# Transposing gathered expert rows on VectorE and ScalarE instead of TensorE, in a float32 mixture-of-experts kernel

## The chip, the cores and the metric

The kernel runs on one core of a Trainium2 chip. The metric is device time in microseconds (us) of one execution. Before the change it is 930.4 us, the median of three runs (930.36, 930.40, 931.57). In the text PE is TensorE, DVE is VectorE, ACT is ScalarE, POOL is GpSimd and SP is SyncE.

## What is computed

Four sequences of 1024 tokens of width 512 each pass through one linear layer, chosen per sequence from 64 by a category number. A router then sends every token to the best of 8 experts, at most 512 tokens to each. An expert is two matrices with a ReLU between them (512 to 2048 to 512). Its output, scaled by the router's probability, is added to the token's original `x`. Everything is float32.

```python
xc = einsum('bsd,bdh->bsh', x, W[cat]) + b[cat][:, None, :]
probs = softmax(xc @ Wr);  eidx = argmax(probs);  p_tok = probs[eidx]
rank = how many earlier tokens chose the same expert;  keep = rank < 512
for e in range(8):
    xe = xc[tokens of e]                      # 512 x 512
    h  = maximum(xe @ W1[e], 0)               # 512 x 2048
    y[tokens of e] += (h @ W2[e]) * p_tok
out = x + y
```

## The kernel before

**Two stages.** The first stage (up to about 149 us) transposes `x`, computes the linear layer and the router, and writes the layer's result to two DRAM tensors `xc_dram` (left and right half of the columns). It also writes, for each slot of each expert, which token sits there. The second stage works through experts `e = 0` to `7`, each some 96 us long.

**Seven products instead of eight.** All large products use a Strassen-Winograd scheme: the operands are cut in quarters, DVE forms sums and differences of quarters (`sums`, `differences`), and seven products, numbered `k = 1` to `7`, are accumulated in three PSUM banks called x, y and z. Product 1 opens bank x; ACT takes a snapshot of the bank (line 761), and products 6 and 7 are then accumulated onto it, with a snapshot after each. So product 6 may only begin when snapshot `s1` has been copied, 7 when `s6` has, and 4 when `s7` has. Each bank has two buffers.

**One expert.** Its 512 rows are gathered by POOL (`gather`, line 691) into four tiles of 128 rows, in two halves of 256 columns each. PE transposes them (`transpose_rows`, line 719) into a PSUM tile, ACT copies that to the tile `xe` (line 720; for expert 0 DVE does), and DVE adds three blocks of differences (lines 729 to 733). The first layer then runs over four groups `g = 0..3` of 512 hidden columns, with seven products of 1.73 us of PE time in each group: 1, 2, then 4 and 3 of the group before, then 6, 5, 7. `first_layer` ends with the bank totals on DVE (line 765), the ReLU on ACT (line 766, and line 773 for product 4) and, after product 3, the DVE sums of `h` (lines 160 to 163). Of the second layer three products run whole (`second_layer(e, 1)`, `6`, `7`, each 6.9 us of PE time), and products 2, 5, 3 and 4 are cut in quarters once more and run as 7 small products each (`small`, `inner_product`, line 856, 0.89 us each), after DVE has formed their `inner_sums`. Results are added to the tile `residual` (gathered rows of the original `x`) by `add`, a DVE `scalar_tensor_tensor` (line 791), and POOL scatters the finished rows to the output (line 889).

**What sets the order.** PE and SP run in the order of the program text (`manual_schedule`). On ACT, DVE and POOL a planner decides at build time: it takes the earliest instruction in the program that it believes to be ready. Each engine then runs its list strictly in that order. `behind` and `issue_after` force a place after a given instruction, and `soon` (`high_priority`) puts an instruction ahead of others that are ready. `fetch(e)`, called in group 1 of expert `e`, gathers the residual rows of `e` and then the rows of expert `e + 1`. For expert 0 the groups 0 and 1 are interleaved, so its `fetch` comes late, and at that time three large copies of `x` to the output (line 920) are under way.

**Where the transposes of the next expert stand.** They are woven between the small products of the present one by `ahead`: one tile before product (2,1), two before (2,4), one after (5,2).

```python
second_layer(e, 6)
inner_sums(e, 5)
ahead(0)
small(*[(2, q) for q in (1, 5, 2, 6, 3, 7)])
ahead(1, 2)
small((2, 4))
inner_sums(e, 3)
second_layer(e, 7)
inner_sums(e, 4)
small((5, 5), (5, 2))
ahead(3)
```

**The start.** SP issues the four loads of the first `x` chunk, then (line 211) the first weights, whose address depends on the category number; ACT issues the router weights and the clearing of `slots`. PE runs three idle matmuls (`keep_warm`, each two passes) before the first transposes of `x`.

Of the kernel before, what the change touches and what calls it, by code (L numbers as in the profile page):

```python
# [8 lines left out]
F32 = mybir.dt.float32  # L9
# [7 lines left out]
P = 128  # L17
# [5 lines left out]
def kernel(  # L23
# [29 lines left out]
    W1G = 3  # L53
    NS = E * SC
    Q = 32
    ROW = 2
# [5 lines left out]
    w1p = ctx.enter_context(tc.tile_pool(name="w1p", bufs=W1G))  # L62
    xg = ctx.enter_context(tc.tile_pool(name="xg", bufs=SC))

# [5 lines left out]

    latest = [None]

    def behind(f, *at):
# [9 lines left out]
    def unordered(group, ins):  # L83
# [8 lines left out]
    make_identity(nc, ident)  # L92
    idle = const.tile([P, D], F32, name="idle")
    nc.vector.memset(idle, 0.0)
    wr_sb = const.tile([P, KC, Q], F32, name="wr_sb")
    nc.vector.memset(wr_sb, 0.0)
    nc.scalar.dma_start(
        out=wr_sb[:, :, 0:E], in_=wr.rearrange("(kc p) e -> p kc e", p=P)
    )
    zeros = const.tile([P, T * ROW // P], F32, name="zeros")  # L100
    nc.vector.memset(zeros, 0.0)
    slots = dram.tile([T, ROW], F32, name="slots")
    nc.scalar.dma_start(out=slots.rearrange("(p s) r -> p (s r)", p=P), in_=zeros)
    before = const.tile([P, P], F32, name="before")
    make_upper_triangular(nc, before, diag=False)
    ones = const.tile([P, P], F32, name="ones")
    nc.gpsimd.memset(ones, 1.0)
# [15 lines left out]
    AHEAD = GT // 2  # L123
    scan = [const.tile([P, AHEAD + GT, E], F32, name=f"scan_{i}") for i in range(2)]
    for t in scan:
        nc.vector.memset(t, 0.0)
    wrc = [const.tile([P, KC, Q], F32, name=f"wrc_{b}") for b in range(B)]
    for t in wrc:
# [60 lines left out]
    with (  # L189
# [54 lines left out]

        def load_x(c):
            t = xin.tile([P, XT, D], F32, tag="x", name=f"x_{c}")
            n = 1 if c == 0 else XT
            for j in range(0, XT, n):
                nc.sync.dma_start(
                    out=t[:, j : j + n, :],  # L250
                    in_=xf[c * CT + j * P : c * CT + (j + n) * P, :].rearrange(
                        "(j p) d -> p j d", p=P
                    ),
                )
            xrows[c] = t
# [365 lines left out]
        with tc.manual_schedule(engines={mybir.EngineType.PE, mybir.EngineType.SP}):  # L621
            load_x(0)
            load_batch(0)
            load_x(1)
            load_batch(1)
            load_x(2)
            load_batch(2)
            keep_warm(ps_t, 3)
            for i in range(XT):
                transpose_x(0, i)  # L630
            for b in range(B):
                for i, product in enumerate(ORDERS[b]):
                    linear(*(b, *product)[-3:])
                    for f, *at in loads.get((b, i), []) + beside.get((b, i), []):
                        f(*at)
# [7 lines left out]
        for row, *ops in ((src_row, float(T - 1), ALU.add, ALU.min), (dst_row, None, ALU.add)):  # L643
            nc.gpsimd.tensor_scalar(
                row.rearrange("p (e c) -> p e c", c=SC), token, FAR, *ops
            )


# [33 lines left out]
    def gather(e, pool, sources, into, at):  # L682

        n = D // len(sources)
        for j, source in enumerate(sources):
            for c in range(SC):
                if j == 0:
                    into[e * SC + c] = pool.tile(
                        [P, D], F32, tag="rows", name=f"rows_{e * SC + c}"
                    )  # L690
                nc.gpsimd.indirect_dma_start(  # L691
                    out=into[e * SC + c][:, j * n : (j + 1) * n],
                    out_offset=None,
                    in_=source,
                    in_offset=bass.IndirectOffsetOnAxis(ap=at[:, c : c + 1], axis=0),
                )

    def fetch(e):

        at = rowp.tile([P, 2 * SC], I32, tag="at", name=f"at_{e}")  # L700
        n = min(2 * SC, NS - e * SC)
        nc.vector.tensor_copy(at[:, 0:n], src_row[:, e * SC : e * SC + n])  # L702
        gather(e, xr, [xf], residual, at[:, 0:SC])
        if e + 1 < E:
            gather(e + 1, xg, xc_dram, rows, at[:, SC : 2 * SC])

    def transpose_rows(e, c, parts=range(2)):

        if e not in xes:
            xes[e] = xep.tile([P, 7, HK, HC * P], F32, tag="xe", name=f"xe_{e}")  # L710

        t = xes[e]
        r = rows[e * SC + c]
        half, at = divmod(c, HC)
        n = len(parts)
        lo = parts[0] * HK
        ps = ps_e.tile([P, KC, P], F32, tag="t", name=f"ps_e_{e}_{c}_{lo}")
        for kc in range(n * HK):
            nc.tensor.transpose(ps[:, kc, :], r[:, (lo + kc) * P : (lo + kc + 1) * P], ident)
        (nc.vector.tensor_copy if e == 0 else nc.scalar.copy)(  # L720
            t[
                :, 2 * half + parts[0] : 2 * half + parts[0] + n, :, at * P : (at + 1) * P
            ].rearrange("p b k n -> p (b k) n"),
            ps[:, 0 : n * HK, :],
        )
        if c == SC - 1:
            b11, b21, b12, b22, t1, t2, t4 = (t[:, k, :, :] for k in range(7))
            if 0 in parts:
                nc.vector.tensor_tensor(t1, b12, b11, ALU.subtract)
            if 1 in parts:  # L730
                nc.vector.tensor_tensor(t2, b22, t1, ALU.subtract)
                nc.vector.tensor_tensor(b12, b22, b12, ALU.subtract)
                nc.vector.tensor_tensor(t4, b21, t2, ALU.subtract)

# [5 lines left out]
    def first_layer(e, g, k):  # L740
# [16 lines left out]
        if k in (1, 6, 7):  # L757
            banks[key, k] = snap.tile(
                [P, HB, HC * P], F32, tag=f"s{k}", bufs=2, name=f"s{k}_{e}_{g}"
            )  # L760
            nc.scalar.copy(banks[key, k], ps)  # L761

# [23 lines left out]

    def add(e, ps, half, at, columns):

        row = residual[e * SC + half * HC + at][:, columns]
        with tc.high_priority():  # L790
            nc.vector.scalar_tensor_tensor(  # L791
                row, ps, table[:, half * HC + at, e, 0:1], row, ALU.mult, ALU.add
            )

    def second_layer(e, k):
# [55 lines left out]
    def inner_product(e, k, q):  # L851
# [13 lines left out]
        half, part = CORNERS[k][0]  # L865
        if len(CORNERS[k]) == 1:
            lo = part * HD + n * P
            add(e, ps, half, at, slice(lo, lo + P))
        else:
            if (e, k) not in whole:  # L870
                whole[e, k] = snap.tile([P, HC, HD], F32, tag="whole", name=f"p{k}_{e}"), set()
            t, begun = whole[e, k]
            into = t[:, at, n * P : (n + 1) * P]
            if (at, n) in begun:
                soon(nc.vector.tensor_tensor, into, ps, into, ALU.add)
            else:
                nc.scalar.copy(into, ps)
            begun.add((at, n))
            banks[e, k, "parts"] = banks.get((e, k, "parts"), 0) + 1
            if banks[e, k, "parts"] == 7:  # L880
                for half, part in CORNERS[k]:
                    for i in range(HC):
                        add(e, t[:, i, :], half, i, slice(part * HD, (part + 1) * HD))

# [37 lines left out]
    with tc.manual_schedule(engines={mybir.EngineType.PE, mybir.EngineType.SP}):  # L922
        gather(0, xg, xc_dram, rows, src_row)

        for part, half, then in (
            ([0], 0, [(0, 1)]),
            ([0], 1, [(1, 1), (0, 5), (1, 5)]),
            ([1], 0, [(0, 2)]),
            ([1], 1, [(1, 2)]),
        ):  # L930
# [6 lines left out]
        for e in range(E):  # L937
            for g in range(NG):
# [7 lines left out]
                first_layer(e, g, 1)  # L946
                first_layer(e, g, 2)
                between(e, g)
                first_layer(e, g, 6)
                first_layer(e, g, 5)  # L950
                first_layer(e, g, 7)
            second_layer(e, 1)
# [7 lines left out]
            def small(*turns):  # L960
                for k, q in turns:
                    inner_product(e, k, q)

            def ahead(*tiles):
                for c in tiles:
                    if e + 1 < E:
                        transpose_rows(e + 1, c)

            second_layer(e, 6)
            inner_sums(e, 5)  # L970
            ahead(0)
            small(*[(2, q) for q in (1, 5, 2, 6, 3, 7)])
            ahead(1, 2)
            small((2, 4))
            inner_sums(e, 3)
            second_layer(e, 7)
            inner_sums(e, 4)
            small((5, 5), (5, 2))
            ahead(3)
            small(  # L980
# [37 lines left out]
```

## Time and profile before

| what | value |
|---|---|
| median of three runs | 930.4 us |
| the profiled execution's own time | 930.86 us |
| its span in the trace | 929.1 us |
| first stage | 0 to about 148.8 us |
| one expert in the steady state (293.46 to 389.70) | 96.24 us |
| granted PE clock | 0.998 |
| transposes of gathered rows, line 719 | 128 instructions, 16 for each expert |
| copies of them on ACT, line 720 | 28, mean 588 ns |
| busy in the span: DVE, ACT, POOL | 70%, 21%, 20% |

A group line of the profile names the line, the engine, the operation, the tile written and the tiles read, the shapes and the count; then its busy time and the mean duration; then how long the engine idled before such instructions and for what. Since matmuls are pipelined, the duration of one of them is longer than the distance from its start to the start of the next. The cost of a matmul is read from the starts in the timeline.

### The profile page before, as it was taken

To read this page: it belongs to the slowest core of one execution; us is meant where nothing else is said; L and a number is where in the kernel's file an instruction comes from. 1 tells how busy PE (TensorE), PEld (TensorE's weight loads), DVE (VectorE), ACT (ScalarE), POOL (GpSimd) and SP (SyncE) were. 2 spreads that over 40 slices of the span, in tenths; PEclk is the share of its full clock that TensorE was granted. 3 is DMA by queue.
4 is the path that set the end of the run, shared out by engine and by line. 5 is a ranking of instruction groups with operands and counts; after the bars stand their busy time and mean duration, and the time that the engine had idled before them with its cause. 6 is when DMAs were issued, how large, how long until landed. Compare 5 with 4: busy or idle time off the path is not lost.

```text
span 929.1 us, 13272 instructions
## 1 busy us (share of the span) xinstructions
PE 915.9 (99%) x5318; PEld 817.5 (88%) x5318; DVE 654.9 (70%) x1222; ACT 193.5 (21%) x350; POOL 181.7 (20%) x173
## 2 busy tenths in 40 slices
PE   9999999999999999999999999999999999999996
PEld 6788787889988998899889988999889988998886
DVE  4656684589549954987488847883789368945793
ACT  3323200321132103210331023112311132113200
POOL 0043443060141013201230024001500150012001
PEclk9999999999999999999999999999999999999999
DMA  8475223992372118310841085106520562044001
GB/s 299 157 242 167 81 80 117 343 379 90 100 254 100 46 61 266 127 47 21 275 152 46 1 277 164 58 1 227 182 91 2 202 202 90 2 154 159 1 1 46
DMA packets 95727, 123.32 MB, mean 133 GB/s; under 512 B 8516, under 2 KB 83268, under 8 KB 95474
## 3 DMA queue, kind: packets, MB, share of 16 engines
q1 hardware_dynamic: 85634, 97.54, 31.5%
q0 software_dynamic: 9216, 24.85, 8.1%
q8 instruction: 42, 0.69, 0.3%
q10 hardware_dynamic: 816, 0.08, 0.1%
q14 instruction: 19, 0.16, 0.1%
HBM read 105.96 MB, written 25.23 MB: 141 GB/s over the span
## 4 chain that ended last, share of the span: by engine, by line
PE 64%; issue 18%; DVE 13%; POOL 3%; DMA 1%; ACT 0%; POOLq 0%; DVEq 0%
PE hx L746 19%; PE hy L746 9%; PE yx L856 7%; PE xcx_lin L488 6%; PE hz L746 5%; PE yx L803 4%; PE yy L856 3%; DVE rows L791 2%; PE xcy_lin L488 2%; POOL rows L691 2%; DVE h L160 2%; DVE h L161 2%; PE ps_xT L273 1%; PE xcz_lin L488 1%; DVE h L163 1%
## 5 line engine op out<-in xcount | busy, mean ns | idle before, releaser
L746 PE MATMUL hx<-xe,w 128*128 128x256 f32 x1024 | 237.7, 379 | 1.2 <-DVE xe L720 1.0
L746 PEld LDWEIGHTS hx<-xe,w 128*128 128x128 f32 x1024 | 193.8, 190 | 27.7 <-DVE xe L720 1.2
L889 POOL DMA_INDIRECT out_dram<-rows,dst_row x32 | 32.0, 999 | 465.3 <-DVE rows L791 428.6
L746 PE MATMUL hy<-xe,w 128*128 128x256 f32 x512 | 120.6, 379 | 0.0
L803 PE MATMUL yx<-w_b,h 128*128 128x256 f32 x512 | 113.1, 379 | 0.0
L746 PEld LDWEIGHTS hy<-xe,w 128*128 128x128 f32 x512 | 97.3, 190 | 13.2
L803 PEld LDWEIGHTS yx<-w_b,h 128*128 128x128 f32 x512 | 96.7, 190 | 12.8
L761 ACT COPY s<-hx 128x512 f32<-128x512 f32 x96 | 55.8, 582 | 222.7 <-PE hx L746 222.7
L765 DVE TENSOR_TENSOR h<-hy,s 128x512 f32<-128x512 f32 x64 | 44.1, 688 | 76.0 <-PE hy L746 51.7
L766 ACT ACTIVATE h<-h 128x512 f32<-128x512 f32 x96 | 60.5, 630 | 150.7 <-DVE h L765 150.7
L856 PE MATMUL yx<-w_b,h 128*128 128x128 f32 x640 | 83.4, 275 | 0.7 <-DVE rows L791 0.6
L791 DVE SCALAR_TENSOR_TENSOR rows<-yx,table,rows 128x128 f32<-128x128 f32 (+1 forms) x160 | 59.9, 398 | 30.8 <-PE yx L856 30.7
L856 PEld LDWEIGHTS yx<-w_b,h 128*128 128x128 f32 x640 | 77.3, 192 | 1.1 <-DVE rows L791 1.0
L691 POOL DMA_INDIRECT rows<-in_x_dram,at x32 | 45.2, 1412 | 145.4 <-DVE at L702 106.2
L691 POOL DMA_INDIRECT rows<-xc_dram,at x56 | 58.4, 1043 | 21.4 <-issue 14.3
L746 PE MATMUL hz<-xe,w 128*128 128x256 f32 x256 | 60.6, 379 | 0.6 <-DVE xe L720 0.6
L765 DVE TENSOR_TENSOR h<-hz,s 128x512 f32<-128x512 f32 x32 | 22.0, 688 | 55.4 <-PE hz L746 55.4
L803 PE MATMUL yx<-w_t,h 128*128 128x256 f32 x256 | 56.6, 379 | 0.0
L460 POOL DMA_INDIRECT slots<-row,dest x32 | 36.3, 1136 | 96.4 <-DVE dest L456 87.9
L746 PEld LDWEIGHTS hz<-xe,w 128*128 128x128 f32 x256 | 48.5, 190 | 7.4 <-DVE xe L720 0.9
L803 PEld LDWEIGHTS yx<-w_t,h 128*128 128x128 f32 x256 | 48.6, 190 | 6.6
L856 PE MATMUL yx<-w_t,h 128*128 128x128 f32 x384 | 52.1, 279 | 0.4
(160 smaller groups left out, 1244.3 us busy)
## 6 DMA issues: line engine op xcount, KB each, us to landing
w<-in_L_ffn_W_dram SPq DMA_DIRECT2D x64, 512.0 KB, 4.3
w_b<-in_L_ffn_W_dram SPq DMA_DIRECT2D x32, 1024.0 KB, 10.9
x<-in_x_dram SPq DMA_DIRECT2D x7, 1024.0 KB, 8.7
xc_dram<-s SPq DMA_DIRECT2D x22, 256.0 KB, 2.7
out_dram<-in_x_dram SPq DMA_DIRECT2D x2, 2816.0 KB, 20.3
cw<-in_L_cond_W_dram SPq DMA_DIRECT2D x3, 1024.0 KB, 10.6
out_dram<-in_x_dram SPq DMA_DIRECT2D x1, 2560.0 KB, 12.2
xc_dram<-xc SPq DMA_DIRECT2D x8, 256.0 KB, 2.3
```

The costliest lines, as they stand in the source:

```text
L160: eng.tensor_tensor(s1, a21, a22, ALU.add)
L460: nc.gpsimd.indirect_dma_start(out=slots, out_offset=bass.IndirectOffsetOnAxis(ap=dest[:, j : j + 1], axis=0), in_=row[:, j, :], in_offset ...
L488: nc.tensor.matmul(ps[:, j, :], lhsT=left[:, kc, j * P : (j + 1) * P], rhs=right[k][:, kc, :], start=((k in OPENS or (b, k) == (LATE, 3)) ...
L691: nc.gpsimd.indirect_dma_start(out=into[e * SC + c][:, j * n : (j + 1) * n], out_offset=None, in_=source, in_offset=bass.IndirectOffsetOnA ...
L746: nc.tensor.matmul(ps[:, j, :], lhsT=w1s[e, g][:, LEFT[k], kc, j * P : (j + 1) * P], rhs=xes[e][:, RIGHT1[k], kc, :], start=(k in OPENS an ...
L761: nc.scalar.copy(banks[key, k], ps)
L765: latest[0] = nc.vector.tensor_tensor(into, ps, part, ALU.add)
L766: nc.scalar.activation(into, into, AF.Relu)
L791: nc.vector.scalar_tensor_tensor(row, ps, table[:, half * HC + at, e, 0:1], row, ALU.mult, ALU.add)
L803: nc.tensor.matmul(ps[:, at, :], lhsT=hs[e][:, m // HB, LEFT[k], m % HB, at * P : (at + 1) * P], rhs=w2s[e][RIGHT2[k]][:, m, :], start=(k ...
L856: nc.tensor.matmul(ps, lhsT=left[:, g, :], rhs=right[:, g, :], start=(q in OPENS and g == 0), stop=(q == LAST[BANK[q]] and g == NG - 1), s ...
L889: nc.gpsimd.indirect_dma_start(out=of, out_offset=bass.IndirectOffsetOnAxis(ap=dst_row[:, n : n + 1], axis=0), in_=residual.pop(n), in_off ...
```

## The change

Expert 0's rows are still transposed by PE. For experts 1 to 7 PE no longer takes part:

- `regroup(e + 1, a)` is called four times in the last group of expert `e`. Each call issues four ACT copies. One copy moves 32 partitions of the gathered rows (512 elements in each) to another 32 partitions of a new tile `strips`. All sixteen together put 32x32 blocks where a blockwise transpose needs them.
- `turn(e + 1)` transposes the 32x32 blocks with four DVE instructions of 128x512 elements, straight into `xe`. `sum_xe` then forms the three difference blocks as before.
- The eight gathers of expert `e + 1` go to one tile with one buffer, and `fetch` issues them before the residual gathers of `e`, not after.
- `second_layer(e, 7)` moves ahead of small product (2,4).
- Small products of 2, 3 and 4 are no longer added to `residual` one by one. Of seven, three are copied by ACT to a buffer `whole`, three are added to it by DVE, one is added directly; the buffer is then added to `residual` in two pieces. Adds straight from PSUM keep their high priority, those from the buffer lose it.
- Snapshots `s1` and `s7` have one buffer instead of two.
- At the start ACT's queue issues the four loads of the first `x`, then the router weights and the clearing of `slots`; SP goes straight to the weights. `keep_warm` runs two idle matmuls instead of three. Constants of the first stage move to a pool `early` that is closed before the second.

```diff
+    early = early_on.enter_context(tc.tile_pool(name="early", bufs=1))
...
-            load_x(0)
+            load_x(0, nc.scalar)
             load_batch(0)
+            nc.scalar.dma_start(
+                out=wr_sb[:, :, 0:E], in_=wr.rearrange("(kc p) e -> p kc e", p=P)
+            )
+            nc.scalar.dma_start(out=slots.rearrange("(p s) r -> p (s r)", p=P), in_=zeros)
...
-            keep_warm(ps_t, 3)
+            keep_warm(ps_t, 2)
...
-        gather(e, xr, [xf], residual, at[:, 0:SC])
         if e + 1 < E:
             gather(e + 1, xg, xc_dram, rows, at[:, SC : 2 * SC])
+        gather(e, xr, [xf], residual, at[:, 0:SC])
...
+    def regroup(e, a):
+        if (e, "strips") not in rows:
+            rows[e, "strips"] = xep.tile(
+                [P, KC, SC, VB, V], F32, tag="strips", name=f"strips_{e}"
+            )
+        r = rows[e, "all"][a * V : (a + 1) * V].rearrange("p s (k b v) -> p s k b v", b=VB, v=V)
+        for b in range(VB):
+            into = rows[e, "strips"][b * V : (b + 1) * V, :, :, a, :]
+            with tc.issue_after(snapped[0].ins):
+                nc.scalar.copy(into.rearrange("p k s v -> p s k v"), r[:, :, :, b, :])
+
+    def turn(e):
+        t = rows.pop((e, "strips"))
+        for half in range(2):
+            for j in range(2):
+                nc.vector.transpose(
+                    xe_of(e)[:, 2 * half + j, :, :],
+                    t[:, j * HK : (j + 1) * HK, half * HC : (half + 1) * HC, :, :].rearrange(
+                        "p k s a v -> p k (s a v)"
+                    ),
+                )
...
-                [P, HB, HC * P], F32, tag=f"s{k}", bufs=2, name=f"s{k}_{e}_{g}"
+                [P, HB, HC * P], F32, tag=f"s{k}", bufs=1 + (k == 6), name=f"s{k}_{e}_{g}"
             )
-            nc.scalar.copy(banks[key, k], ps)
+            snapped[0] = nc.scalar.copy(banks[key, k], ps)
...
+        single = len(CORNERS[k]) == 1
+        if single and q == 4:
+            add(e, ps, half, at, columns(n * P, P))
         else:
...
+            if (at, n) in done:
                 soon(nc.vector.tensor_tensor, into, ps, into, ALU.add)
             else:
                 nc.scalar.copy(into, ps)
+            done.append((at, n))
+            if not single:
+                if len(done) == 7:
+                    for corner, part in CORNERS[k]:
+                        for i in range(HC):
+                            add(e, t[:, i, :], corner, i, columns(0, HD), urgent=False)
+            elif at == 1 and done.count((1, 1)) == 2:
+                add(e, into, half, 1, columns(P, P), urgent=False)
+            elif at == 0 and done.count((0, 0)) == done.count((0, 1)) == 2:
+                add(e, t[:, 0, :], half, 0, columns(0, HD), urgent=False)
...
                 first_layer(e, g, 1)
                 first_layer(e, g, 2)
+                if e + 1 < E and g == NG - 1:
+                    regroup(e + 1, 0)
                 between(e, g)
-                first_layer(e, g, 6)
-                first_layer(e, g, 5)
-                first_layer(e, g, 7)
+                for i, k in enumerate((6, 5, 7)):
+                    first_layer(e, g, k)
+                    if e + 1 < E and g == NG - 1:
+                        regroup(e + 1, i + 1)
...
             inner_sums(e, 5)
-            ahead(0)
             small(*[(2, q) for q in (1, 5, 2, 6, 3, 7)])
-            ahead(1, 2)
+            second_layer(e, 7)
             small((2, 4))
             inner_sums(e, 3)
-            second_layer(e, 7)
             inner_sums(e, 4)
+            if e + 1 < E:
+                turn(e + 1)
             small((5, 5), (5, 2))
-            ahead(3)
+            if e + 1 < E:
+                sum_xe(e + 1)
```

## The prediction

> **What bounds the kernel.** I read the page first: the busy shares, the granted clock and the chain that ended last.
>
> ```profile
> span 929.1 us, 13272 instructions
> PE 915.9 (99%) x5318; PEld 817.5 (88%) x5318; DVE 654.9 (70%) x1222; ACT 193.5 (21%) x350; POOL 181.7 (20%) x173
> PEclk9999999999999999999999999999999999999999
> PE 64%; issue 18%; DVE 13%; POOL 3%; DMA 1%; ACT 0%; POOLq 0%; DVEq 0%
> ```
>
> PE is busy throughout at full clock. A busy PE could still hide gaps, so I went on to the stretches of single experts. Columns: length, then busy time and count for PE, weight loads, DVE, ACT and POOL, then clock, DMA share, GB/s.
>
> ```profile
> 389.70:485.94 96.24, 96.19 (x561) 87.67 (x561) 70.88 (x126) 19.85 (x36) 17.43 (x16) 1.00 0.36 119
> 871.00:929.10 58.10, 49.81 (x337) 46.34 (x335) 38.39 (x77) 3.51 (x8) 3.99 (x4) 0.97 0.05 19
> ```
>
> A steady expert has 0.05 us of idle PE in 96.24. So time is saved only by taking instructions from PE, and lost only where PE gets a new wait. DVE (70.88) and ACT (19.85) have room on average; whether they have it at the right moment is the question.
>
> **What the transposes cost PE.** From PE's timeline, small products (2,7), two transposed tiles, and (2,4):
>
> ```profile
> 411.70 1.06 PE L856 MATMUL yx<-w_b,h 128*128 128x128 f32 x8
> 412.60 1.04 PE L719 MATMUL ps_e<-ident,rows 128*128 128x128 f32 x8
> 413.47 1.06 PE L856 MATMUL yx<-w_b,h 128*128 128x128 f32 x8
> ```
>
> Durations overlap, so I take starts: eight transposes hold PE for 413.47 − 412.60 = 0.87 us, 0.109 each. An expert has 16 (1.74 us), seven experts 112: **−12.2 us**.
>
> The Trainium skill ("VectorE: DVE Perf Modes", The three transpose paths, and its rules for kernel authors) speaks against the change: a full 128x128 transpose belongs on TensorE, at 390 ns in bf16, since VectorE turns only 32x32 blocks. Its 390 ns would make 112 x 0.39 = 43.7 us gained; it is the time of one alone, and the row shows 0.109 us in a stream. The row decides. The rule also leaves out which engine is full; its warning about 32x32 blocks is paid here by ACT's copies.
>
> **The work that replaces them.** The nearest rows (all 512 elements per partition):
>
> ```profile
> L720 ACT COPY xe<-ps_e 128x512 f32<-128x512 f32 x28 | 15.7, 588 | 80.2 <-PE ps_e L719 80.2
> L731 DVE TENSOR_TENSOR xe<-xe 128x512 f32<-128x512 f32 x8 | 5.5, 692 | 0.3
> ```
>
> *ACT.* Sixteen copies of 512 elements per partition. At 588 ns that is 9.4 us per expert, less four removed copies (2.35), plus nine small-product copies at 266 ns (2.4): 29 of 94 us busy. Fewer partitions should not shorten a copy; strides in runs of 32 might lengthen it. Bounds 0.5 to 1.2 us; I take 0.59. Their place matters, because PE waits for snapshots (ACT's timeline, group 3):
>
> ```profile
> 482.57 0.59 ACT L761 COPY s<-hx 128x512 f32<-128x512 f32 x1 [0.42 <-PE hx L746]
> 486.03 0.59 ACT L761 COPY s<-hx 128x512 f32<-128x512 f32 x1 [2.87 <-PE hx L746]
> ```
>
> These are `s6` and `s7`. `s1` ends at 476.57; four copies fill 476.6 to 478.9, and the next ReLU starts at 478.94 anyway. `s6` stays at 482.57, needed by product 7 at 484.05. Eight copies follow (483.2 to 487.9), so `s7` ends near 488.5 instead of 486.6; product 4 of group 3 needs it only at 492.68. No PE wait: **0**. If this cover goes, it costs what the slower rival below works out.
>
> *DVE.* Four transposes at the row's 0.69 (0.60 apart) add 2.4 us. The lower bound is 0.5 each; the upper, twice the row, adds 2.4 us more. The seven adds (348 ns) of each of products 2, 3, 4 become one add, three sums (286 ns), and two adds from the buffer (348 and 482): 2.03 instead of 2.44 us, −1.2 per expert. From 429 to 444 us DVE idles half the time, and `xe` is needed only at 439. **0** either way.
>
> *Banks.* The ACT copies and short sums release PSUM sooner. Product (5,1) needs the bank of `second_layer(7)`; its four adds ended 2.2 us after that layer, and (2,4), (5,5), (5,2) lie between now (2.7 us). Expert 7, with no transposes to cover it, waited 0.25 us at (2,7) and 0.83 at (2,4); now `second_layer(7)` precedes (2,4): **−0.8**, bounds 0 and −1.1. Tiny waits of at most 0.4 us per expert elsewhere I leave (bounds ±2 in all).
>
> *Answered shortly.* One buffer for `s1` and `s7`: their readers end before the next snapshot; in expert 0 group 1's `s1` must wait for the total at 159.6 to 160.3, and its next product comes at 163.6, so 0. The `early` pool's readers end before `xe` is first written at 148, so 0. Scatters and the end of the kernel do not move.
>
> **The start.**
>
> ```profile
> 1.14 1.81 SPq L249 DMA_DIRECT2D x<-in_x_dram  x4
> 3.99 1.56 SPq L211 DMA_DIRECT2D cw<-in_L_cond_W_dram  x3
> 5.88 0.23 PEld L273 LDWEIGHTS ps_xT<-ident,x 128*128 128x128 f32 x1 [0.52 <-issue]
> 12.18 0.69 DVE L502 TENSOR_TENSOR s<-xcx_lin,cb 128x512 f32<-128x512 f32 x1 [0.64 <-DMA cb<-in_L_cond_b_dram]
> ```
>
> The first transposes follow the idle matmuls, not the load. One idle matmul less is two passes of 0.855 us, 1.7 us. ACT issues six DMAs at about 0.45 us (0.7 to 3.4), then loads its table (1.28): free before the first copy. SP loses 1.81 us of issuing, but its next instruction still waits for the category number, so weights, bias and all later loads on SP come 0 to 1 us earlier. The bias holds the fourth row and, behind it on DVE, the sums that PE's product at 14.64 needs; the gain cannot much exceed the bias's shift.
>
> Here the skill's page "TensorE: Matmul & The Clock Gate" (The HAM clock gate) weighs against the cut: warm-up is some 3.4 us of busy time, not a number of matmuls, so transposes moved forward run cold. The trace agrees in part: the first ones took 421 ns, later ones 273. By the row alone the gain is 1.7; by the rule half the 16 transposes (0.9 us) run at half speed and 0.8 is left. I take **−0.9**, bounds 0 and −1.7.
>
> **Expert 0, the new wait.**
>
> ```profile
> 187.72 1.75 POOL L691 DMA_INDIRECT rows<-in_x_dram,at  x1 [31.81 <-issue]
> 203.74 0.87 DVE L791 SCALAR_TENSOR_TENSOR rows<-yx,table,rows 128x256 f32<-128x256 f32 x2
> 206.82 7.07 PE L803 MATMUL yx<-w_t,h 128*128 128x256 f32 x32
> 209.13 0.69 DVE L161 TENSOR_TENSOR h<-h 128x512 f32<-128x512 f32 x1
> 210.65 1.19 POOL L691 DMA_INDIRECT rows<-xc_dram,at  x1 [4.62 <-DMA rows<-in_x_dram,at]
> 203.19 11.29 DMA rows<-xc_dram,at
> ```
>
> For later experts gathers land in about 3.8 us, and there is time: the last row gather would issue near 372 and land near 376, ACT wants it at 380; residuals land near 383, DVE wants them at 396. Here gathering begins at 187.7 under copies of `x`: the third gather landed at 210.6 (the fifth row shows who waited for it), the fourth by 212.1, the ninth (last row) at 214.5. With rows first, the eight row gathers hold the bytes of the former four and land near 211.5; the first two residual tiles near 214. But DVE wants these at 203.74, and everything behind the add on DVE waits too: the total of product 3, then the sums (209.13, ending 209.8) that `second_layer(0, 6)` needs for its last quarter at 206.8 + 5.2 = 212.0. DVE's chain would shift by 214.5 − 204.6 = 9.9 us; 2.2 us of slack and 0.6 of idle DVE come off: PE waits about 7 us. If the planner puts that add behind the sums, the wait is 0 to 2. ACT's copies can block too: if they stand ahead of the two ReLUs of products 4 and 3 (207.7), those start at 211.5 + 16 x 0.55 = 220.3 and PE waits about 11. Bounds 0 and 12; I take **+6**, near the add's row and a little below, for the order is unknown.
>
> **The sum.** 930.86 (profiled execution: span 929.1 and 1.76 around it) − 12.2 − 0.9 − 0.8 + 6 = 923.0. The median lies 0.46 lower: **922.5 us**.
>
> **Rivals.**
>
> *No wait in expert 0.* The planner takes other ready work first on DVE and ACT, or loads come earlier. For it: ready work waits at 203 to 209 (weight sums, totals). Against: the add has high priority, and a planner cannot know the slow landings. 930.4 − 13.9 = **916.5 us**.
>
> *The full block on ACT in expert 0.* 16 copies ahead of the ReLUs: 930.4 − 13.9 + 11 = **927.5 us**. For it: the copies stand earlier in the program than these ReLUs. Against: the planner may already expect the rows late.
>
> *Slower: copies too slow on ACT, in every expert.* `s7` stands behind eight copies. From 483.16 to 492.68 there is room for 8c + 0.8, so PE waits once a copy takes c > 1.09 us; the gain of 7.9 us that is left in the forecast is eaten when the wait is 1.1 us per expert, at c = 1.23. At c = 1.6 the wait for `s6` (1.3 us) and for `s7` (4.8) are 6.1 us in each of seven experts: 922.5 + 43 = **965 us**. For it: copies across partitions in runs of 32 appear in no row. Against: 588 ns for 512 elements is a rate per element, and nothing suggests twice that.
>
> **Numbers.** Forecast (a wait of 4 to 9 us) 0.45, no wait 0.30, full block 0.15, slow copies 0.10. A measurement here tells 0.2%, 1.9 us, from no change. Faster takes the first two and half the third: 0.82. Same: 0.06, slower: 0.12. The range runs from the rival without a wait, with the start and small waits at their good ends (912.5), to the full block with unlucky small terms (930); left out are the slow copies and edges.
>
> **What would show it.** Line 719 with 16 instructions instead of 128. Experts 1 to 6 at about 94.5 us, with PE idle near 0. Copies of `strips` at 0.55 to 0.65 us, DVE transposes at 0.6 to 0.7. A PE gap near 210 to 220 us, and DVE waiting for a residual DMA before it (or ACT for the rows). Product (0,0,1) of the first stage near 8.5 us instead of 9.4. I am wrong if a steady expert is not shorter by about 1.7 us, or if PE waits for `s6` or `s7`.

## The result, and the profile after

The changed kernel takes 937.6 us, the median of four runs (936.94 to 938.49), against 930.7 in runs of the kernel before on the same chip. The ratio is 1.0073, with a 95% interval of 1.0056 to 1.0091: slower by about 7 us. The forecast was 922.5 us, with a range of 912.5 to 930.

Below are the lines of the changed kernel's page that answer to those shown of before.

```profile
span 935.2 us, 13219 instructions
PE 902.6 (97%) x5204; PEld 807.9 (86%) x5204; DVE 660.5 (71%) x1226; ACT 264.9 (28%) x506; POOL 176.9 (19%) x173
...
PEclk9999999978999999999999999999999999999999
...
PE 93%; DVE 2%; DMA 2%; POOL 1%; issue 1%; ACT 0%; POOLq 0%; DVEq 0%
```

PE's busy time fell by 13.3 us (915.9 to 902.6), and yet the span grew by 6.1. So PE stands idle somewhere. The clock row says where to look: the slices of some 23 us that are not full are the ninth and the tenth, 187 to 234 us. That is expert 0. A steady expert and the last part, by the stretches view (columns as before: length, busy time and count of PE, weight loads, DVE, ACT, POOL; clock, DMA share, GB/s):

```profile
313.18:407.40 94.22, 94.22 (x546) 86.07 (x545) 71.90 (x127) 29.73 (x58) 16.91 (x16) 1.00 0.38 123
878.40:935.20 56.80, 49.43 (x337) 46.30 (x335) 37.01 (x74) 5.89 (x17) 3.99 (x4) 0.98 0.05 19
```

There the change does what it was forecast to do, and a little more: 94.22 us for an expert instead of 96.24, with PE never idle, and 56.80 instead of 58.10 at the end. The view of waits (total, times, longest) has one long wait of PE:

```profile
PE hx L787 <- ACT s L802: 21.4, 1, 21.4
```

PE waits once, for a snapshot of ACT, and longer than the whole steady gain. The timeline of that place (start, duration, engine, line, operation, tiles; in brackets the idle time before it and its releaser):

```profile
186.34 1.81 POOL L704 DMA_INDIRECT rows_of<-xc_dram,at  x1 [31.73 <-DVE w L163]
188.50 0.58 ACT L814 ACTIVATE h<-hx 128x512 f32<-128x512 f32 x1
...
199.86 0.95 POOL L704 DMA_INDIRECT rows_of<-xc_dram,at  x1 [0.30 <-issue]
...
211.25 2.50 ACT L747 COPY strips<-rows_of 32x512 f32<-32x512 f32 x4 [22.17 <-DMA rows<-in_x_dram,at]
213.78 0.63 ACT L807 ACTIVATE h<-h 128x512 f32<-128x512 f32 x1
214.31 0.57 ACT L802 COPY s<-hx 128x512 f32<-128x512 f32 x1
214.44 0.69 DVE L163 TENSOR_TENSOR h<-h 128x512 f32<-128x512 f32 x1 [20.70 <-ACT h L807]
...
214.93 3.78 PE L787 MATMUL hx<-xe,w 128*128 128x256 f32 x8 [21.36 <-ACT s L802]
```

It reads from the bottom up. Product 7 of group 3 waits for `s6` (line 802, at 214.31). `s6` and a ReLU of group 2 stand behind the four copies of `regroup(1, 0)` on ACT's list. These copies wait for the gathered rows, and ACT, idle since 189.1, does nothing else for 22 us. The rows are so late because POOL begins to gather at 186.3 and issues the last row gather at 199.9, and because that one takes about 11 us to land. (The bracket names a residual gather as the releaser. The copies read `rows_of`, and it is the rows that they need; the two kinds of gather land side by side.)

The last row holds one thing more: the eight matmuls take 3.78 us, where they took 1.89. After the gap the clock is down. Three stretches, the gap and what follows:

```profile
193.57:214.93 21.36, 0.00 (x1) 0.00 (x1) 0.66 (x2) 3.59 (x7) 9.49 (x10) 0.62 0.82 300
214.93:219.00 4.07, 4.07 (x10) 3.27 (x11) 4.00 (x8) 4.00 (x7) 0.00 (x0) 0.50 0.00 0
219.00:222.00 3.00, 3.00 (x15) 2.67 (x14) 1.28 (x2) 2.92 (x6) 0.00 (x0) 0.98 0.00 0
```

PE runs at a granted clock of 0.50 for about 4 us: product 7 and the first matmuls of `second_layer(0, 1)` cost 2.2 us more. The Trainium skill ("TensorE: Matmul & The Clock Gate", The HAM clock gate) has this rule: half clock after an idle window of some 3.4 us, full clock again after about as long a busy one. By it an estimate is half of 3.4, 1.7 us; the rows give 2.2. The term was missing in the forecast's price of a wait.

The spans then add up:

| place | us |
|---|---|
| first stage, its end at 147.52 instead of 148.84 | −1.3 |
| experts 0 to 6, 7 x 2.02 | −14.1 |
| last part, 58.10 to 56.80 | −1.3 |
| wait for `s6` in expert 0 | +21.4 |
| half clock after it | +2.2 |
| rest, in expert 0 (0.4 of it: before, PE waited there for gathered rows) | −0.8 |
| sum, as the spans (929.1 to 935.2) | +6.1 |

### The profile page after: what moved, and what is told of

Same layout as the page of the kernel before. It is cut to its first block, busy times and chain, and to the rows that moved or that the text cites. A ratio compares the mean times of both kernels' runs of the same rounds, so it can differ in the third digit from the quotient of the medians.

```text
span 935.2 us, 13219 instructions
## 1 busy us (share of the span) xinstructions
PE 902.6 (97%) x5204; PEld 807.9 (86%) x5204; DVE 660.5 (71%) x1226; ACT 264.9 (28%) x506; POOL 176.9 (19%) x173
## 4 chain that ended last, share of the span: by engine, by line
PE 93%; DVE 2%; DMA 2%; POOL 1%; issue 1%; ACT 0%; POOLq 0%; DVEq 0%
PE hx L787 23%; PE yx L848 18%; PE yx L901 12%; PE hy L787 11%; PE yy L901 6%; PE xcx_lin L491 6%; PE hz L787 5%; PE yz L901 3%; PE xcy_lin L491 2%; PE ps_xT L276 2%; PE xcz_lin L491 1%; DMA rows_of<-xc_dram,at 1%; POOL rows_of L704 1%; PE ps_lT L382 1%; PE ps_wT L330 1%
## 5 line engine op out<-in xcount | busy, mean ns | idle before, releaser
L787 PE MATMUL hx<-xe,w 128*128 128x256 f32 x1024 | 239.6, 382 | 22.5 <-ACT s L802 21.4
L848 PEld LDWEIGHTS yx<-w_b,h 128*128 128x128 f32 x512 | 97.3, 191 | 12.8
L704 POOL DMA_INDIRECT rows_of<-xc_dram,at x56 | 63.1, 1127 | 140.7 <-DVE w L164 94.0
L747 ACT COPY strips<-rows_of 32x512 f32<-32x512 f32 x112 | 69.0, 616 | 23.6 <-DMA rows<-in_x_dram,at 22.2
L163 DVE TENSOR_TENSOR h<-h 128x512 f32<-128x512 f32 x64 | 43.7, 683 | 22.1 <-ACT h L807 22.1
```

The lines of the kernel that those rows point to most:

```text
L163: eng.tensor_tensor(s1, a21, a22, ALU.add)
L704: nc.gpsimd.indirect_dma_start(out=into[e * SC + c][:, j * n : (j + 1) * n], out_offset=None, in_=source, in_offset=bass.IndirectOffsetOnA ...
L747: nc.scalar.copy(into.rearrange("p k s v -> p s k v"), r[:, :, :, b, :])
L787: nc.tensor.matmul(ps[:, j, :], lhsT=w1s[e, g][:, LEFT[k], kc, j * P : (j + 1) * P], rhs=xes[e][:, RIGHT1[k], kc, :], start=(k in OPENS an ...
L848: nc.tensor.matmul(ps[:, at, :], lhsT=hs[e][:, m // HB, LEFT[k], m % HB, at * P : (at + 1) * P], rhs=w2s[e][RIGHT2[k]][:, m, :], start=(k ...
```

## The experiments

The theory: one wait in expert 0 costs 23.6 us (21.4 and 2.2), from ACT's fixed order and rows that come late, and everything else in the change is a gain of about 17. The rivals: the wait that the forecast chose, a DVE `add` that waits for residual rows; the copies of `x` to the output, which crowd the DMA; the copies on ACT, too long in every expert; and that the edits of the small products do nothing, or harm.

Every ratio below is against the kernel before on the same chip, in brackets the 95% interval.

**The place on ACT's list: behind `s7`.** For expert 1 all regroup calls move behind `second_layer(0, 6)` in the program.

```diff
-                if e + 1 < E and g == NG - 1:
+                if 0 < e and e + 1 < E and g == NG - 1:
                     regroup(e + 1, 0)
...
             second_layer(e, 6)
+            if e == 0:
+                for a in range(VB):
+                    regroup(1, a)
             inner_sums(e, 5)
```

> The regroup copies for expert 1 alone move behind the second layer's product 6 in the program; on ScalarE's list they now stand behind snapshots s6 and s7 but ahead of the ReLUs of products 4 and 3. Theory A (the loss is one wait: ScalarE stands still for expert 1's gathered rows with s6 queued behind): TensorE no longer waits for s6 at 193.6 us; rows land near 211 us, 15 copies of 0.62 us run to 220.6, then the ReLUs and two sums, so TensorE waits about 12 us near 211 to 223 instead of 21.4 at 193.6; 926 to 929 us. Rival B (the copies cost TensorE or VectorE time all along, or the clock lost in the second stage is not due to the wait): no change from 937.6.

Measured: 930.8 us, 0.9996 (0.9989 to 1.0002). That is 6.8 us less than the changed kernel, but more than was expected. The wait for `s6` is gone, and two others are there: 7.8 us before `second_layer(0, 6)` and 5.5 within it. The first is the forecast's wait. The second is the rival "full block": the planner still put the copies ahead of the two ReLUs of products 3 and 4. ACT's timeline, and PE's second wait:

```profile
211.81 1.25 ACT L747 COPY strips<-rows_of 32x512 f32<-32x512 f32 x2 [15.48 <-DMA rows<-in_x_dram,at]
213.07 0.63 ACT L807 ACTIVATE h<-h 128x512 f32<-128x512 f32 x1
213.71 8.14 ACT L747 COPY strips<-rows_of 32x512 f32<-32x512 f32 x13
221.87 0.60 ACT L814 ACTIVATE h<-hx 128x512 f32<-128x512 f32 x1
222.49 0.61 ACT L747 COPY strips<-rows_of 32x512 f32<-32x512 f32 x1
223.13 0.63 ACT L807 ACTIVATE h<-h 128x512 f32<-128x512 f32 x1
...
226.26 3.78 PE L848 MATMUL yx<-w_t,h 128*128 128x256 f32 x8 [5.47 <-DVE h L164]
```

The last quarter of `second_layer(0, 6)` needs the `h` sums, these need the last ReLU (223.13), and that stands behind all sixteen copies (2, 13 and 1).

**The place on ACT's list: behind the last ReLU.** As above, and for expert 1 the copies are also held behind the latest ReLU.

```diff
-            with tc.issue_after(snapped[0].ins):
+            with tc.issue_after((relu if e == 1 else snapped)[0].ins):
...
-            nc.scalar.activation(into, into, AF.Relu)
+            relu[0] = nc.scalar.activation(into, into, AF.Relu)
```

> As e1, but the copies for expert 1 are held behind the last ReLU of expert 0's first layer. Theory A: nothing on TensorE's path stands behind them on ScalarE. What remains is VectorE's add, which wants the residual rows that are gathered last: they land near 213 us, and VectorE's queue behind it costs TensorE about 7 to 8 us near 211 to 218; 921 to 923 us. If the residual rows are not waited for, 914. Rival B: 937.

Measured: 925.3 us, 0.9934 (0.9918 to 0.9951), some 2 us more than expected. Now only the forecast's wait is left, and the timeline shows it alone:

```profile
212.27 0.48 DVE L834 SCALAR_TENSOR_TENSOR rows<-yx,table,rows 128x256 f32<-128x256 f32 x1 [10.11 <-DMA rows<-in_x_dram,at]
213.00 0.48 DVE L834 SCALAR_TENSOR_TENSOR rows<-yx,table,rows 128x256 f32<-128x256 f32 x1 [0.25 <-DMA rows<-in_x_dram,at]
...
213.54 10.19 PE L849 MATMUL yx<-w_t,h 128*128 128x256 f32 x32 [8.23 <-DVE rows L834]
```

The add waits for a residual gather until 212.3, and PE waits 8.2 us for the adds. The product is late at its start, not at its last quarter: product 6 is accumulated onto the bank that these adds have to read first. Half clock then costs 3.1 us more (10.19 instead of 7.07). So this wait is real, worth 11 us; in the changed kernel it was hidden behind the longer one.

**The rows earlier.** The gathers for expert 1 are called ahead of the loads of expert 0's second weights, as soon as PE has transposed expert 0's own rows.

```diff
+        fetch(0)
         load_w2(0, xes[0][:, 3, 0, HC * P - 1 :])
...
-        if g == 1:
+        if g == 1 and e > 0:
             behind(fetch, e)
```

> Expert 0's fetch (its residual rows and expert 1's rows) is called before its second-layer weights are loaded, some 25 us earlier, before the copies of x to the output begin. Theory A: both gathers land by about 180 us, no wait in expert 0: the start's 1.3, seven experts at 2.0 each and 1.3 at the end remain, 930.7 - 16.8 = 914 us. Rival B: 935 or more. Against A in part: if the gathers slow the weights' load, VectorE waits for weights near 178 us and some 1 to 5 us come back.

Measured: **914.2 us**, 0.9814 (0.9798 to 0.983). It beats both kernels, by 1.9% and 2.5%, with every other part of the change in place and ACT's copies where the planner puts them. Two lines of its page:

```profile
PE 900.2 (99%) x5204; PEld 804.5 (88%) x5204; DVE 660.6 (72%) x1226; ACT 264.9 (29%) x506; POOL 172.5 (19%) x173
...
PEclk9999999999999999999999999999999999999999
```

The row gathers are issued from 159.8 to 168.7 and land in 6.2 us at the median. ACT's first copies start at 187.0 without waiting for them. This run settles the theory: only the time of the gathers differs from the changed kernel, so the late rows alone turned 17 us of gain into 7 of loss.

**Fewer DMAs at that time.** The three copies of `x` to the output are left out of the changed kernel, so rows of tokens that no expert takes are not written.

```diff
-            nc.sync.dma_start(out=of[q, :], in_=xf[q, :])
+            if g > NG:
+                nc.sync.dma_start(out=of[q, :], in_=xf[q, :])
```

> Leaves out the three copies of x to the output, so rows of tokens that no expert takes are not written. It separates the two reasons for the late landing: the fetch being issued late (186.3 us), and the DMA queues being full. If congestion is nearly all of it, rows land near 200 us (eight issues of 1.25 us from 186.3, then 3.7 us), TensorE waits for s6 until about 203.5 us, 10 us instead of 21.4: about 925 us. If lateness does not come from congestion, landing stays near 211 and the time near 937; if congestion were everything, no wait and 914.

Measured: 929.3 us, 0.9977 (0.9968 to 0.9986). The wait shrinks, and doesn't go:

```profile
203.46 2.50 ACT L747 COPY strips<-rows_of 32x512 f32<-32x512 f32 x4 [14.32 <-DMA rows_of<-xc_dram,at]
...
207.14 3.78 PE L787 MATMUL hx<-xe,w 128*128 128x256 f32 x8 [13.51 <-ACT s L802]
```

Of ACT's 22.2 us, 7.9 were crowding and 14.3 the late issue. The eight row gathers now land in 3.2 us at the median (11.4 in the changed kernel), but they are issued as late as before. POOL's first three issues still take 1.8, 3.2 and 3.2 us, where most take 0.95; that is 5.4 of the 14.3. I had put these down to the output copies, and expected some 4 us less. DVE runs sums of 128x1024 elements (1.2 us each) beside them, but no run moves those away; what slows the issues stays open.

**The old order of the gathers.** The changed kernel with the residual rows gathered first.

```diff
+        gather(e, xr, [xf], residual, at[:, 0:SC])
         if e + 1 < E:
             gather(e + 1, xg, xc_dram, rows, at[:, SC : 2 * SC])
-        gather(e, xr, [xf], residual, at[:, 0:SC])
```

> The changed kernel with the residual rows gathered first, as before the change. By its list ScalarE now takes s6 ahead of all copies but s7 behind twelve. Rows land near 214.5 us, twelve copies take 7.5, s7 ends near 222.6, and product 4 of group 3 wants it at 202: TensorE waits about 20 us there, and VectorE's add finds its rows: 936 us, about the changed kernel's time. If only the wait for s6 mattered: 917.

Measured: 935.7 us, 1.0053 (1.0038 to 1.0068), as expected. The rows then come at 213.9, twelve copies stand ahead of `s7` instead of four ahead of `s6`, and PE waits 19.9 us. The order of the two kinds hardly matters; that both begin at 186 does.

**The start alone.** The kernel before, with the loads of `x` on ACT's queue and two idle matmuls.

```diff
-            load_x(0)
+            load_x(0, nc.scalar)
             load_batch(0)
+            nc.scalar.dma_start(
+                out=wr_sb[:, :, 0:E], in_=wr.rearrange("(kc p) e -> p kc e", p=P)
+            )
+            nc.scalar.dma_start(out=slots.rearrange("(p s) r -> p (s r)", p=P), in_=zeros)
...
-            keep_warm(ps_t, 3)
+            keep_warm(ps_t, 2)
```

> The kernel before with only the edits of the start: first x through ScalarE's queue, router weights and clearing of slots behind it, two idle matmuls. Theory: the first expert product of the changed kernel came 1.3 us earlier than before (147.5 against 148.8), and this is worth the same alone: 929.4 us against 930.7. Rival: the later loads take it back: 930.7.

Measured: 929.4 us, 0.9989 (0.9983 to 0.9996): −1.4 us between the medians, with an interval of about −0.4 to −1.6. That agrees with the 1.3 us by which the first stage ends sooner. How many of the first 16 transposes of `x` are slow (about 400 ns or more, 273 later) differs between the traces: four before, eleven in the changed kernel, one here.

**Twice the copies.** The early-fetch version, in which each regroup copy is made twice. It sizes the slower rival, copies too slow on ACT.

```diff
-                nc.scalar.copy(into.rearrange("p k s v -> p s k v"), r[:, :, :, b, :])
+                for _ in range(2):
+                    nc.scalar.copy(into.rearrange("p k s v -> p s k v"), r[:, :, :, b, :])
```

> The kernel with the early fetch (e3), each regroup copy made twice, so that one costs 1.25 us. By the cover worked out in the prediction, snapshot s7 behind eight doubled copies ends about 1 us after product 4 wants it in each of seven experts, s6 just in time: 914.2 + 7 = 921 us. If ScalarE had room for it: 914. If more than that stands behind the copies: 930 or more.

Measured: 940.6 us, 1.0104 (1.0089 to 1.012); the expectation missed by 20 us. The step itself is there, a little larger than its formula gives: `s7` comes behind sixteen copies, and PE waits 1.9 us in each of seven experts.

```profile
390.73 10.14 ACT L748 COPY strips<-rows_of 32x512 f32<-32x512 f32 x16
400.90 0.58 ACT L803 COPY s<-hx 128x512 f32<-128x512 f32 x1
...
401.54 1.99 PE L788 MATMUL hx<-xe,w 128*128 128x256 f32 x8 [1.87 <-ACT s L803]
```

That is 13.1 us of the 26.5 lost against the early fetch. Another 3 are waits of 0.3 to 0.4 for DVE in small products, and PE's busy time, grown from 900.2 to 909.9, holds the rest. Half clock accounts for 5.1 of it: three of the seven waits are followed by 3.41 us at 0.50. What the other 4.6 are is said below the table.

**The small products as before.** The early-fetch version with single adds one by one and `second_layer(e, 7)` behind (2,4).

```diff
-        if single and q == 4:
+        if single:
             add(e, ps, half, at, columns(n * P, P))
...
-            second_layer(e, 7)
             small((2, 4))
             inner_sums(e, 3)
+            second_layer(e, 7)
```

> The kernel with the early fetch (e3), but small products are added to the residual rows one by one and product 7 of the second layer follows (2,4), as before the change. Theory: a steady expert took 94.22 us where 1.74 us of transposes taken from 96.24 leave 94.50, and the last part was 1.3 us shorter; both are the buffers' and the new place's work, so this run loses 7 x 0.28 + 1.1 = 3 us: 917. Rival: these waits went with the transposes: 914.

Measured: 928.1 us, 0.9971 (0.9961 to 0.9981), where 914 to 917 was expected. Moving the transposes off PE, with the small products left as they were, gains 3 us of a possible 17. A steady expert takes 96.0 us again, for PE now waits at two small products in each:

```profile
411.49 1.16 PE L901 MATMUL yx<-w_b,h 128*128 128x128 f32 x8 [0.45 <-DVE rows L833]
...
431.17 1.16 PE L901 MATMUL yx<-w_b,h 128*128 128x128 f32 x8 [0.86 <-DVE rows L833]
```

PE's transposes had been time in which DVE emptied the banks. Without them PE comes to (2,4) 1.3 us sooner (three of four tiles, 12 x 0.109), and DVE has the new transposes in its queue too. How much each of the two costs was not tried apart.

**Buffers and place, one at a time.** Two more versions with the early fetch: the new place of `second_layer(e, 7)` without the buffers (the first diff), and the buffers with the old place (the second).

```diff
-        if single and q == 4:
+        if single:
```

```diff
-            second_layer(e, 7)
             small((2, 4))
             inner_sums(e, 3)
+            second_layer(e, 7)
```

> The early-fetch kernel (e3) with small products added one by one as before, but product 7 of the second layer in its new place ahead of (2,4). In e7 TensorE waited twice per expert for single adds that stood in VectorE's full queue (0.45 and 0.86 us idle). Theory: the buffers, not the place, take these waits away, so this stays near e7: 926 to 928 us. Rival: the place did it: 914 to 916.

> The complement: buffers as changed, product 7 back behind (2,4). Theory: 914 to 916 us. Rival (the place did it): 926 to 928.

Measured: 944.7 us, 1.0119 (1.0084 to 1.0153), for the place alone, and 927.0, 0.9943 (0.9922 to 0.9965), for the buffers alone. The first lies 16 us and more above both expectations, the second is what its rival expected. One wait per expert tells the first story; the views are the timeline of the version without buffers and, in columns as before, two of its stretches:

```profile
434.92 0.35 DVE L833 SCALAR_TENSOR_TENSOR rows<-yx,table,rows 128x128 f32<-128x128 f32 x1
435.32 0.97 PEld L901 LDWEIGHTS yx<-w_b,h 128*128 128x128 f32 x8 [2.08 <-DVE rows L833]
435.32 1.16 PE L901 MATMUL yx<-w_b,h 128*128 128x128 f32 x8 [1.89 <-DVE rows L833]
436.32 1.79 PE L901 MATMUL yz<-w_t,h 128*128 128x128 f32 x8
```

```profile
433.03:436.44 3.41, 1.52 (x14) 1.33 (x13) 2.22 (x7) 0.00 (x0) 0.00 (x0) 1.00 0.00 0
436.44:439.85 3.41, 3.41 (x19) 3.41 (x18) 0.70 (x2) 0.00 (x0) 0.00 (x0) 0.50 0.00 0
```

Adds from banks and from buffers share one queue of DVE, and the add that would empty PE's next bank stands behind four from a buffer (432.99 to 435). The wait of 1.89 is 13.2 us in seven experts, and after five of the seven the matmuls run at half clock for 3.41 us (1.79 instead of 1.06). The four runs of this version spread from 939.6 to 946.5, and the fastest has the higher mean clock (0.995, the others 0.987 or 0.988). In the other version, with the buffers and the old place, a sum of 0.28 us stands behind a longer one on DVE, which has been busy without a break since 400.0, and PE waits 0.7 for it at (2,4). Two lines of that version's waits (total, times, longest):

```profile
PE yx L901 <- DVE p L88: 5.4, 8, 0.7
PE hx L787 <- issue: 4.3, 6, 1.0
```

The second line is a wait that neither theory has, and the version without buffers has it too (3.6 us). In five experts ACT takes a snapshot `s6` 1.7 us late, and PE waits 0.6 to 0.7 us for it (the sixth time is in expert 0). The profile shows no instruction that held ACT up, so the cause stays open. Both edits together leave PE without any of these waits.

**The buffers in the kernel before.** Both edits of the small products, and one buffer for `s1` and `s7`, with PE still transposing; `small` is as in the change.

```diff
+            second_layer(e, 7)
             small((2, 4))
             inner_sums(e, 3)
-            second_layer(e, 7)
...
-                [P, HB, HC * P], F32, tag=f"s{k}", bufs=2, name=f"s{k}_{e}_{g}"
+                [P, HB, HC * P], F32, tag=f"s{k}", bufs=1 + (k == 6), name=f"s{k}_{e}_{g}"
```

> The kernel before with only the small-product edits: buffers, product 7's new place and, for room, one buffer each for s1 and s7. TensorE still transposes. Theory: with the transposes in place the waits on single adds were hidden but for 0.4 us per expert and 1.1 in the last one, so the edit alone is worth 1 to 4 us: 927 to 930. Rival: it is worth the 13.9 us that it is worth beside the moved transposes: 917.

Measured: 930.6 us, 0.9988 (0.998 to 0.9996), a gain of 0.8 us between the medians (0.4 to 1.9 by the interval). With PE's transposes as cover the same edits are worth nearly nothing; without it, 13.9 (928.1 against 914.2).

**All of them in one table.** A span is PE's busy time plus its idle time. So each version must lose, against the early fetch, about its PE waits plus the busy time that PE has above 900.2 us; the table shows where each loss lies. "Of it clock" is worked out from the granted clock: PE's busy time in stretches of 1 us, times the share of the clock that was not granted.

| version | PE waits | busy above 900.2 | of it clock | sum | measured above 914.2 |
|---|---|---|---|---|---|
| the change | 21.4 | 2.4 | 2.1 | 23.8 | 23.4 |
| behind `s7` | 13.3 | 3.6 | 3.8 | 16.9 | 16.6 |
| behind the ReLUs | 8.6 | 2.6 | 3.1 | 11.2 | 11.1 |
| no output copies | 13.5 | 3.0 | 2.6 | 16.5 | 15.2 |
| residual rows first | 19.9 | 2.4 | 2.0 | 22.3 | 21.5 |
| twice the copies | 16.0 | 9.7 | 5.1 | 25.7 | 26.5 |
| small products as before | 9.7 | 3.4 | 0.0 | 13.1 | 13.9 |
| no buffers, new place | 16.8 | 13.5 | 8.5 | 30.3 | 30.5 |
| buffers, old place | 9.7 | 3.4 | 0.0 | 13.1 | 12.8 |

All sums agree within 1.3 us. Where one or two long waits make the loss, the busy time grows by half clock alone, within 0.5 us. Where there are many short waits, it grows at full clock too: by 3.4 us in "small products as before" (15 waits) and in "buffers, old place" (14), some 0.24 us a wait. Matmuls overlap, and each wait breaks the overlap: the small product after one takes 1.16 us instead of 1.06. Without a cause are the waits for the late `s6`: 3.6 us of the 16.8 in "no buffers, new place" and 4.3 of the 9.7 in "buffers, old place".

## Why the prediction was wrong

**The step that failed** is "Expert 0, the new wait", at +6 with bounds 0 and 12; it measured 23.6. Two things in it were wrong. First, the place on ACT's list. Its worst case put the sixteen copies ahead of the ReLUs at 207.7; in truth four of them stood ahead of `s6`, due at 193, so ACT stopped at 189.1, 18.6 us earlier than the worst case allowed. Second, the sentence that made this impossible, "No PE wait: 0" for `s6` and `s7`. It was worked out from a steady expert, where the rows have landed before ACT reaches the copies, and was then used for expert 0, where they had not. The landing itself was right: 211.5 forecast, 211.25 measured.

**The sign of failure** was named rightly: "I am wrong", it says, "if PE waits for `s6` or `s7`". PE did.

**The chosen mechanism was there, only covered.** With ACT out of the way the add waits for a residual gather until 212.3 and PE waits 8.2 us, 7 forecast (6 taken); but at the product's start, and with 3.1 us of half clock, which the sum did not have.

**The rivals.** "Full block" named the right mechanism at the wrong place: behind `s7` it shows as 5.5 us next to the 7.8. "No wait", at 916.5, is what the early fetch gives, at 914.2. "Slower: copies too slow" does not hold: a copy takes 616 ns, 590 taken, and the steady experts have no wait. Its formula was half right. At 1.27 us a copy it gives 10.1 + 0.8 − 9.5 = 1.4 us of wait, and 1.9 was measured; but later waits and the lost clock make that 3.8 us per expert (26.5 / 7), more than the 2.4 that an expert's share of the gain is. The formula had the gain about used up there, so the true limit is likely lower than its 1.23; it wasn't tried.

**The other terms** were close, and the three gains were all forecast too small:

| term | forecast | measured |
|---|---|---|
| transposes, with the small waits left aside | −12.2 | −14.1 |
| start | −0.9 | −1.3 |
| banks, expert 7 | −0.8 | −1.3 |
| ACT copy of 32x512, each | 0.59 us | 0.62 us |
| DVE transpose, each | 0.69 us | 0.69 us |

One term was right by luck: DVE's added work at "0 either way". DVE had time on average, but the runs without one of the two small-product edits show that it lacked the time at the banks. The forecast gave these edits 0.8 us; the gain of 14 rests on both. It had the sign before it: expert 7, "with no transposes to cover it", waited 0.25 us at (2,7) and 0.83 at (2,4), and with the small products as before a steady expert waits at (2,4) too (0.45), and at a later one (0.86).

**The range** was too narrow on its upper side because its end was the worst case of one place, and the place was the unknown.

## What to carry to other kernels

An instruction that waits for a DMA stops all that stands behind it on its engine (here ACT, for 22 us): put copies of fetched data into an in-order list only where the slowest landing of any round, the first one included, lies before them. The steady state gives the gain and the first round can give the loss, so work both out, each with its own landings. And work taken from the full engine also takes away the time in which others emptied its buffers (the same two edits were worth 0.8 us with the transposes on PE and 13.9 without): look for what was due during it.

## What the runs showed of the hardware

- **Short waits can halve the clock too, where they fall into one slot of a fixed grid.** In the version without buffers the clock is at 0.50 for 3.41 us after five of the seven waits of 1.89 us, and these stretches start 98.99 us apart, 29 steps of 3.413. The two stretches above are neighbours on that grid: PE idle for 1.89 of 3.41 us (55%), then 0.50. With twice the copies three of seven waits of 1.9 us end so. Of the six waits in the two traces that don't, four are cut by the grid, so that no slot is idle for more than 48%; two lie whole in one slot and keep full clock all the same, which stays open. The rule cited above, an idle window of 3.4 us, would let all fourteen pass. The same section says that the window runs freely, and the grid agrees with that.
- **A copy of 32 partitions costs as much as one of 128.** ACT takes 616 ns for 32x512 between partitions and 588 for 128x512 from PSUM before the change.
- **DVE turns 32x32 blocks at the price of a sum:** 694 ns for 128x512, as for a `tensor_tensor` of that size (692 before the change).
- **Gathers under large copies land slowly:** 11.4 us at the median, 3.2 when the three copies of `x` are left out.
